# Layer norm statistics with five small VectorE operations to a pair of batches, and the second bias by TensorE in 3 of 16 batches

## The chip, the core and the metric

The kernel runs on one core of a Trainium2 chip. The metric is the device time of one execution in microseconds. A core has TensorE (PE, with its weight loads listed as PEld), VectorE (DVE), ScalarE (ACT), GpSimd (POOL) and SyncE (SP, which issues nearly all of the DMAs here). They run at the same time, each through its own list of instructions in order, and wait for each other through semaphores.

## What is computed

There are 128 batches of 128 rows with 512 columns, float32. Each batch has a language id 0 to 8, which picks its weights and its bias rows:

```
h = relu(x @ W1[id] + b1[id])          # 512 -> 128
y = x + h @ W2[id] + b2[id]            # 128 -> 512
n = (y - mean(y)) * rsqrt(var(y) + 1e-5)
out = x + n * gamma[id] + beta[id]
```

## The kernel before

At the start all weights are loaded into SBUF, and the rows of beta, gamma and b2 are spread over the 128 partitions: the rows lie as bfloat16 parts in `parts`, a column of the 0/1 tile `pick` selects one, a matmul copies it to all partitions (`spread`), and VectorE or ScalarE copies the result into `beta_b`, `gamma_b` and `b2_b`.

Then one iteration `i` of the main loop works on several batches at once, each in another stage. The order of each engine's instructions is the order of the calls (`keep` forbids a change).

- TensorE: `transpose_x(i)` (4 instructions, L191), `down(i-1)` (8, L214), `up(i-2)` (2, L231). Where `b2_by_matmul` holds, `up` has one more bfloat16 matmul ahead (L230) that puts the b2 row into the same accumulation.
- ScalarE: copies the transposed x out of PSUM (`copy_xT`, L195), copies the batch's W1 to a fixed place (`stage_w1`, L186), `relu` (L222), the sum of squares (`square`, L249), and once in two batches the square root (`deviation`, L255).
- GpSimd: `add_b2(b+2)` makes r = x + b2 (L201) where TensorE doesn't add b2, and `add_beta(b)` makes o = x + beta (L208). Here b = i - 3. GpSimd reads and writes SBUF in both.
- VectorE, three long instructions to a batch: `residual` adds x or r to the result in PSUM and gives the row sum (L237), `scale` computes (y - mean) * gamma in place (L281), `finish` computes o + y * rstd (L290).

VectorE has small instructions between them. Batches are handled in pairs `g` (even batch, odd batch), and the statistics of a pair have two columns. To a pair there are two times `negative_mean` (L242, one column each), and five instructions for 1/sqrt (L260, L264, L267, L270, L275): the reciprocal of ScalarE's square root and one Newton step. Intermediate results of these lie in PSUM (`stat`), others in SBUF.

Buffers tie the engines together. `p_y` has five PSUM tiles: `up(n)` waits until `finish(n-5)` has read its tile. `rp` has four tiles for r: `add_b2` waits for the `residual` that frees one. `op` has five pairs of o, freed by the stores. `xp` has four groups of four batches of x.

The last batches, from b = 124, are written out by hand in `tail`: statistics by single batch (`rstd_of`, `deviation_of`), part of the last step on ScalarE and GpSimd (`by_pool`, with `shift`, L334, a VectorE product of two SBUF columns), and stores of single batches.

Of the kernel before, what the change touches and what calls it, by code (L numbers as in the profile page):

```python
# [8 lines left out]
FP = mybir.dt.float32  # L9
# [14 lines left out]
def cond_resid_kernel(ctx: ExitStack, tc: tile.TileContext, x, itok, W1, b1, W2, b2, gamma, beta, out):  # L24
# [97 lines left out]
    nc.vector.tensor_scalar(lang, lang, 0, L - 1, ALU.max, ALU.min)  # L122


    R = 3 * L
    parts = const.tile([P, H], BF, name="parts")
    nc.vector.memset(parts.bitcast(mybir.dt.uint32), 0)
# [1 line left out]
    both = st.tile([P, R], FP, tag="both", name="both", bufs=1)[:96, :]  # L129
    nc.vector.tensor_tensor(both, ident[:96, 0:R], ident[:96, 32 : 32 + R], ALU.add)  # L130
    nc.vector.tensor_tensor(pick, both, ident[:96, 64 : 64 + R], ALU.add)
    left = rp.tile([P, H], FP, tag="r", name="left")
    nc.vector.tensor_copy(parts[0:R, :], rows[0:R, :])
    nc.vector.tensor_tensor(left[32 : 32 + R, :], rows[0:R, :], parts[0:R, :], ALU.subtract)
# [43 lines left out]
        return lids[g, engine][b % G]  # L178

    def b2_by_matmul(b):  # L180
        return b < 4 or b % 4 == 1

    def stage_w1(b):
        w1s[b] = wp.tile([P, KC, A], FP, tag="w1s", name=f"w1s_{b}")
# [12 lines left out]
    def add_b2(b):  # L197
        if not b2_by_matmul(b):
            rs[b] = rp.tile([P, H], FP, tag="r", name=f"r_{b}")
            v = lid(b, ET.Pool)  # L200
            keep(nc.gpsimd.tensor_tensor(rs[b], xb(b), b2_b[:, bass.ds(v * H, H)], ALU.add))  # L201

    def add_beta(b):
        g, j = divmod(b, 2)
        if j == 0:
            os[g] = op.tile([P, 2, H], FP, tag="o", name=f"o_{g}")
        v = lid(b, ET.Pool)
        keep(nc.gpsimd.tensor_tensor(os[g][:, j, :], xb(b), beta_b[:, bass.ds(v * H, H)], ALU.add))  # L208
# [15 lines left out]
    def up(b):  # L224
# [6 lines left out]
        keep(nc.tensor.matmul(ys[b], lhsT=hT[b], rhs=w2[:, bass.ds(v * H, H)], start=not m, stop=True))  # L231
        del hT[b]

    def residual(b):
        r = xb(b) if b2_by_matmul(b) else rs.pop(b)
        s = st.tile([P, 1], FP, tag="sum", name=f"sum_{b}")
        keep(nc.vector.scalar_tensor_tensor(ys[b], ys[b], 1.0, r, ALU.mult, ALU.add, accum_out=s))  # L237
        sums[b] = s

    def negative_mean(b):  # L240
        nmeans[b] = st.tile([P, 1], FP, tag="nmean", name=f"nmean_{b}")
        keep(nc.vector.tensor_scalar(nmeans[b], sums.pop(b), -1.0 / H, None, ALU.mult))  # L242

    def square(b):
        g, j = divmod(b, 2)
        if j == 0:
            ssqs[g] = st.tile([P, 2], FP, tag="ssq", name=f"ssq_{g}")
        sq = tp.tile([P, H], FP, tag="sq", name=f"sq_{b}")
        keep(nc.scalar.activation(sq, ys[b], AF.Square, bias=nmeans[b], accum_out=ssqs[g][:, j : j + 1]))  # L249

    sds, y0s, stats = {}, {}, {}

    def deviation(g):
        sds[g] = st.tile([P, 2], FP, tag="sd", name=f"sd_{g}")
        keep(nc.scalar.activation(sds[g], ssqs[g], AF.Sqrt, bias=eps, scale=1.0 / H))  # L255


    def rstd_1(g):
        stats[g] = p_s.tile([P, 6], FP, tag="s", name=f"stat_{g}")
        keep(nc.vector.tensor_scalar(stats[g][:, 0:2], ssqs.pop(g), -0.5 / H, -0.5 * EPS, ALU.mult, ALU.add))  # L260

    def rstd_2(g):
        y0s[g] = st.tile([P, 2], FP, tag="y0", name=f"y0_{g}")
        keep(nc.vector.reciprocal(y0s[g], sds.pop(g)))  # L264

    def rstd_3(g):
        keep(nc.vector.tensor_tensor(stats[g][:, 2:4], stats[g][:, 0:2], y0s[g], ALU.mult))  # L267

    def rstd_4(g):
        keep(nc.vector.tensor_tensor(stats[g][:, 4:6], stats[g][:, 2:4], y0s[g], ALU.mult))  # L270

    def rstd_5(g):
        rstds[g] = st.tile([P, 2], FP, tag="rstd", name=f"rstd_{g}")
        keep(
            nc.vector.scalar_tensor_tensor(rstds[g], stats.pop(g)[:, 4:6], 1.5, y0s.pop(g), ALU.add, ALU.mult)  # L275
        )

    def scale(b):
        v = lid(b, ET.DVE)
        keep(  # L280
            nc.vector.scalar_tensor_tensor(  # L281
                ys[b], ys[b], nmeans.pop(b), gamma_b[:, bass.ds(v * H, H)], ALU.add, ALU.mult
            )
        )

# [11 lines left out]
    def on(b):  # L297
        return 0 <= b < B
# [6 lines left out]
    def rstd_of(b, n):  # L305

        if not ends:
            ends["t"] = p_s.tile([P, 32], FP, tag="s", name="stat_ends")
        t = ends["t"][:, 8 * (b % 4) : 8 * (b % 4) + 3]
        if n == 1:  # L310
            keep(nc.vector.tensor_scalar(t[:, 0:1], ssqs.pop(b), -0.5 / H, -0.5 * EPS, ALU.mult, ALU.add))  # L311
        elif n == 2:
            y0s[b] = st.tile([P, 1], FP, tag="y0", name=f"y0_{b}")
            keep(nc.vector.reciprocal(y0s[b], sds.pop(b)))  # L314
        elif n < 5:
            keep(nc.vector.tensor_tensor(t[:, n - 2 : n - 1], t[:, n - 3 : n - 2], y0s[b], ALU.mult))  # L316
        else:
            rstds[b] = st.tile([P, 1], FP, tag="rstd", name=f"rstd_{b}")
            keep(nc.vector.scalar_tensor_tensor(rstds[b], t[:, 2:3], 1.5, y0s.pop(b), ALU.add, ALU.mult))  # L319

    def deviation_of(b):
        ssq = st.tile([P, 1], FP, tag="ssq", name=f"ssq_{b}")
        sq = tp.tile([P, H], FP, tag="sq", name=f"sq_{b}")
        keep(nc.scalar.activation(sq, ys[b], AF.Square, bias=nmeans[b], accum_out=ssq))
        sds[b] = st.tile([P, 1], FP, tag="sd", name=f"sd_{b}")
        keep(nc.scalar.activation(sds[b], ssq, AF.Sqrt, bias=eps, scale=1.0 / H))
        ssqs[b] = ssq

    def rstd_col(b):
        return rstds[b] if b > E else rstds[b // 2][:, b % 2 : b % 2 + 1]  # L330

    def shift(b):
        ends[b] = st.tile([P, 1], FP, tag="shift", name=f"shift_{b}")
        keep(nc.vector.tensor_tensor(ends[b], nmeans.pop(b), rstd_col(b), ALU.mult))  # L334

    def by_pool(b, scaled):

# [16 lines left out]
    def tail(b):  # L354
        p = E // 2
        if b == E + 3:
            rstd_of(b - 2, 4)
        residual(b)
        if b == E + 1:
            rstd_1(p)  # L360
            rstd_2(p)
            negative_mean(b)
            rstd_3(p)
            scale(E - 1)
            rstd_4(p)
            rstd_5(p)
            shift(E)
            finish(E - 2)
            store(p - 1)
            deviation_of(b)  # L370
            by_pool(E, False)
        elif b == E + 2:
            negative_mean(b)
            rstd_of(b - 1, 1)
            rstd_of(b - 1, 2)
            finish_last(E - 1)
            store_last(E)
            rstd_of(b - 1, 3)
            deviation_of(b)
        elif b == E + 3:  # L380
            rstd_of(b - 2, 5)
            negative_mean(b)
            shift(b - 2)
            residual(b + 1)
            negative_mean(b + 1)
            by_pool(b - 2, False)
            store_last(b - 2)
            rstd_of(b - 1, 1)
            rstd_of(b - 1, 2)
            rstd_of(b - 1, 3)  # L390
            scale(b - 1)
            deviation_of(b)
            rstd_of(b - 1, 4)
            rstd_of(b - 1, 5)
            scale(b)
            deviation_of(b + 1)
            by_pool(b - 1, True)
            store_last(b - 1)
            rstd_of(b, 1)
            rstd_of(b, 2)  # L400
            rstd_of(b + 1, 1)
            rstd_of(b + 1, 2)
            rstd_of(b, 3)
            rstd_of(b + 1, 3)
            scale(b + 1)
            rstd_of(b, 4)
            rstd_of(b + 1, 4)
            rstd_of(b, 5)
            rstd_of(b + 1, 5)
            finish_last(b)  # L410
            finish_last(b + 1)

# [38 lines left out]
    for i in range(3, B + U):  # L451
# [23 lines left out]
        p = g - 1  # L475
        mine, old = 0 <= p < B // 2, 0 <= p - 1 < B // 2
        if b == E:
            for n in range(b + 3, B):
                add_b2(n)
            for n in range(b + 1, B):  # L480
                add_beta(n)
        if b > E:
            tail(b)
        elif half == 0:
            if on(b):
                residual(b)
            if mine:
                scale(2 * p)
            if on(b):
                negative_mean(b)  # L490
            if mine:
                rstd_1(p)
                rstd_2(p)
            if old:
                finish(2 * p - 1)
                store(p - 1)
            if mine:
                rstd_3(p)
        else:
            if on(b):  # L500
                residual(b)
            if mine:
                rstd_4(p)
                scale(2 * p + 1)
                rstd_5(p)
            if on(b):
                negative_mean(b)
            if mine:
                finish(2 * p)
        if 0 <= b <= E:  # L510
            square(b)
# [43 lines left out]
```

## Time and profile before

| | |
|---|---|
| median of 3 runs | 320.62 us (320.58 to 321.12) |
| profiled execution | 321.39 us, span 318.8 us, TensorE clock 0.987 |
| TensorE | busy 305.1 us, 96% of the span |
| VectorE | busy 300.7 us, 94% |
| ScalarE | busy 285.5 us, 90% |
| GpSimd | busy 280.6 us, 88% |
| DMA | 72.88 MB, 16 engines busy 66.4% by the main queue |

The span is the time from the first to the last instruction. The time of the execution is 2.6 us longer, since it takes in what lies around the span. The profiled execution was 0.77 us slower than the median.

A busy share counts the records' durations, and those of instructions that follow each other overlap: the next one starts before the last one's record ends. What an instruction costs its engine in a full queue is the distance from its start to the start of the next, which is shorter than its duration.

### The profile page before, as it was taken

The numbers are of one execution on the slowest core, as the hardware profiler recorded it, in microseconds if no ns is written. First come the engines' busy times: TensorE is split into PE (matmuls) and PEld (weight loads), VectorE is DVE, ScalarE is ACT, GpSimd is POOL, SyncE is SP. The second block draws the span as 40 slices with busy tenths as digits, with TensorE's granted clock in tenths as the row PEclk, the third lists the DMA queues.
The fourth block names the chain that finished last, engine by engine and source line by source line (L and its number), as shares of the span: only waits on it lengthen the run. The fifth ranks groups of instructions, "written<-read, shape, count | busy, mean of one in ns | idle before, by whom it ended". The sixth has DMA issues, their size and how long they took to land. (4 is left out here: it accounts for less than half of the span.)

```text
span 318.8 us, 7184 instructions
## 1 busy us (share of the span) xinstructions
PE 305.1 (96%) x1889; PEld 226.0 (71%) x1889; DVE 300.7 (94%) x1000; ACT 285.5 (90%) x721; POOL 280.6 (88%) x234
## 2 busy tenths in 40 slices
PE   8998999999999999999999999999999999999960
PEld 3475777777777777777777777777777777777730
DVE  5946999999999999999999999999999999999995
ACT  2686989999999999999999999999999999999972
POOL 1306999999999999999999999999999999999873
PEclk9999999999999999999999999999999999999995
DMA  7997577577766666678666676678766666633324
GB/s 204 317 386 288 198 262 254 214 264 263 221 231 212 223 246 232 228 264 263 247 215 213 217 244 231 223 265 264 245 210 215 224 241 228 226 135 133 129 112 156
DMA packets 40986, 72.88 MB, mean 229 GB/s; under 512 B 1737, under 2 KB 6868, under 8 KB 40946
## 3 DMA queue, kind: packets, MB, share of 16 engines
q1 hardware_dynamic: 40886, 72.38, 66.4%
q8 instruction: 15, 0.25, 0.3%
q14 instruction: 25, 0.20, 0.2%
q10 hardware_dynamic: 60, 0.05, 0.1%
HBM read 38.86 MB, written 33.55 MB: 227 GB/s over the span
## 5 line engine op out<-in xcount | busy, mean ns | idle before, releaser
L208 POOL TENSOR_TENSOR o<-x,beta_b 128x512 f32<-128x512 f32 x128 | 162.0, 1278 | 10.6 <-DVE beta_b L160 10.6
L201 POOL TENSOR_TENSOR r<-x,b_b 128x512 f32<-128x512 f32 x93 | 118.8, 1277 | 20.0 <-DMA x<-in_x_dram 12.1
L214 PE MATMUL ph<-xT,w1s 128*128 128x128 f32 x1024 | 135.7, 275 | 0.3 <-ACT w1s L186 0.2
L231 PE MATMUL py<-w,hT 128*128 x256 | 130.9, 593 | 0.2 <-DVE o L290 0.2
L214 PEld LDWEIGHTS ph<-xT,w1s 128*128 128x128 f32 x1024 | 124.6, 192 | 2.6 <-ACT hT L222 1.3
L191 PEld LDWEIGHTS pxT<-ident,x 128*128 128x128 f32 x512 | 63.9, 141 | 67.1 <-issue 43.4
L281 DVE SCALAR_TENSOR_TENSOR py<-py,nmean,gamma_b 128x512 f32<-128x512 f32 x126 | 94.7, 752 | 0.3 <-issue 0.3
L290 DVE SCALAR_TENSOR_TENSOR o<-py,rstd,o 128x512 f32<-128x512 f32 x122 | 90.4, 741 | 1.4 <-DVE nmean L242 0.5
L249 ACT ACTIVATE sq<-py,nmean 128x512 f32<-128x512 f32 x124 | 85.3, 688 | 4.5 <-DVE nmean L242 2.9
L195 ACT COPY xT<-pxT 128x512 f32<-128x512 f32 x128 | 73.8, 577 | 12.1 <-PE pxT L191 10.1
L186 ACT COPY w1s<-w 128x512 f32 x128 | 79.5, 622 | 0.2 <-DVE gamma_b L160 0.2
L191 PE MATMUL pxT<-ident,x 128*128 128x128 f32 x512 | 77.0, 273 | 0.9 <-ACT xT L195 0.7
L237 DVE SCALAR_TENSOR_TENSOR py<-py,r 128x512 f32<-128x512 f32 x93 | 64.7, 695 | 2.5 <-POOL r L201 0.6
L222 ACT ACTIVATE hT<-ph,b1T 128x128 f32<-128x128 f32 x128 | 47.6, 372 | 1.1 <-PE ph L214 1.0
L231 PEld LDWEIGHTS py<-w,hT 128*128 128x128 f32 x256 | 41.6, 192 | 2.9 <-issue 0.9
L237 DVE SCALAR_TENSOR_TENSOR py<-py,x 128x512 f32<-128x512 f32 x35 | 24.2, 692 | 3.7 <-PE py L231 3.7
L249 ACT ACTIVATION_READ_ACCUMULATOR sq<-py,nmean 128x1 f32 x124 | 25.2, 203 | 0.0
L255 ACT ACTIVATE sd<-ssq,eps 128x2 f32<-128x2 f32 x62 | 18.3, 296 | 2.1
L242 DVE TENSOR_SCALAR nmean<-sum 128x1 f32<-128x1 f32 x128 | 18.7, 146 | 0.2
L230 PE MATMUL py<-parts,pick 96*128 96x512 bf16 x35 | 13.3, 381 | 0.0
L237 DVE DVE_READ_ACCUMULATOR py<-py,r 128x1 f32 x93 | 13.1, 141 | 0.0
L270 DVE TENSOR_TENSOR stat<-stat,y 128x2 f32<-128x2 f32 x62 | 12.8, 206 | 0.0
(54 smaller groups left out, 117.7 us busy)
## 6 DMA issues: line engine op xcount, KB each, us to landing
x<-in_x_dram SPq DMA_DIRECT2D x31, 1024.0 KB, 6.1
out_dram<-o SPq DMA_DIRECT2D x61, 512.0 KB, 3.5
w<-in_L_cond_W_dram SPq DMA_DIRECT2D x4, 640.0 KB, 6.6
w<-in_L_cond_W_dram SPq DMA_DIRECT2D x2, 1280.0 KB, 11.5
out_dram<-o SPq DMA_DIRECT2D x6, 256.0 KB, 2.2
x<-in_x_dram SPq DMA_DIRECT2D x2, 512.0 KB, 3.9
rows<-in_L_cond_beta_dram ACTq DMA_DIRECT2D x1, 20.0 KB
rows<-in_L_cond_gamma_dram SPq DMA_DIRECT2D x1, 20.0 KB
```

What stands on the lines that cost most here:

```text
L186: keep(nc.scalar.copy(w1s[b].rearrange("p k a -> p (k a)"), src))
L191: keep(nc.tensor.transpose(pxs[b][:, k, :], xb(b)[:, k * P : (k + 1) * P], ident))
L195: keep(nc.scalar.copy(xT[b], pxs.pop(b)))
L201: keep(nc.gpsimd.tensor_tensor(rs[b], xb(b), b2_b[:, bass.ds(v * H, H)], ALU.add))
L208: keep(nc.gpsimd.tensor_tensor(os[g][:, j, :], xb(b), beta_b[:, bass.ds(v * H, H)], ALU.add))
L214: nc.tensor.matmul(phs[b], lhsT=w1s[b][:, k, :], rhs=xT[b][:, k, :], start=(k == 0), stop=(k == KC - 1))
L222: keep(nc.scalar.activation(hT[b], phs.pop(b), AF.Relu, bias=b1T[:, bass.ds(lid(b, ET.Activation), 1)]))
L231: keep(nc.tensor.matmul(ys[b], lhsT=hT[b], rhs=w2[:, bass.ds(v * H, H)], start=not m, stop=True))
L237: keep(nc.vector.scalar_tensor_tensor(ys[b], ys[b], 1.0, r, ALU.mult, ALU.add, accum_out=s))
L249: keep(nc.scalar.activation(sq, ys[b], AF.Square, bias=nmeans[b], accum_out=ssqs[g][:, j : j + 1]))
L281: nc.vector.scalar_tensor_tensor(ys[b], ys[b], nmeans.pop(b), gamma_b[:, bass.ds(v * H, H)], ALU.add, ALU.mult)
L290: nc.vector.scalar_tensor_tensor(o, ys.pop(b), rstds[g][:, j : j + 1], o, ALU.mult, ALU.add)
```

## The change

Mean, sum of squares and 1/sqrt are computed in another form.

- The sum of a pair goes to two columns of one tile, and `negative_means` makes both means in one instruction, a `tensor_scalar` on 128x2 from SBUF to SBUF, instead of two on 128x1.
- `square` takes the sum itself: it computes (sum - 512 y)^2, 512 squared times too large, so that the scale factors change and ScalarE's square no longer reads the mean.
- 1/sqrt takes one step of Heron: with s the square root from ScalarE and v the variance, 1 / (s + v / s), in four instructions (reciprocal, two `scalar_tensor_tensor`, reciprocal). The factor 2 that this lacks is put into gamma: its columns of `pick` are doubled by one more VectorE instruction at the start. The intermediate columns lie in PSUM, the result in SBUF.
- The order in `tail` is written anew for this.
- `b2_by_matmul` holds for b < 4 and for b % 16 in (1, 6, 11), instead of for b < 4 and b % 4 == 1. That is 27 of the 128 batches, before 35. GpSimd gets the other 101, before 93. One of the last r is made after the last o.

```diff
+    nc.vector.tensor_scalar(pick[:, L : 2 * L], pick[:, L : 2 * L], 2.0, None, ALU.mult)
...
     def b2_by_matmul(b):
-        return b < 4 or b % 4 == 1
+        return b < 4 or b % 16 in (1, 6, 11)
...
+    def col(tiles, b):
+        return tiles[b // 2][:, b % 2 : b % 2 + 1]
...
-    def negative_mean(b):
-        nmeans[b] = st.tile([P, 1], FP, tag="nmean", name=f"nmean_{b}")
-        keep(nc.vector.tensor_scalar(nmeans[b], sums.pop(b), -1.0 / H, None, ALU.mult))
+    def negative_means(g):
+        nmeans[g] = st.tile([P, 2], FP, tag="nmean", name=f"nmean_{g}")
+        keep(nc.vector.tensor_scalar(nmeans[g], sums[g], -1.0 / H, None, ALU.mult))
...
-        keep(nc.scalar.activation(sq, ys[b], AF.Square, bias=nmeans[b], accum_out=ssqs[g][:, j : j + 1]))
+                sq, ys[b], AF.Square, bias=col(sums, b), scale=-float(H), accum_out=col(ssqs, b)
...
     def rstd_1(g):
+        y0s[g] = p_s.tile([P, 6], FP, tag="s", name=f"stat_{g}")
+        keep(nc.vector.reciprocal(y0s[g][:, 0:2], sds[g]))
     def rstd_2(g):
+        keep(nc.vector.scalar_tensor_tensor(t[:, 2:4], ssqs.pop(g), EPS * H3, t[:, 0:2], ALU.add, ALU.mult))
     def rstd_3(g):
+        keep(nc.vector.scalar_tensor_tensor(t[:, 4:6], t[:, 2:4], 1.0 / H3, sds.pop(g), ALU.mult, ALU.add))
     def rstd_4(g):
+        rstds[g] = st.tile([P, 2], FP, tag="rstd", name=f"rstd_{g}")
+        keep(nc.vector.reciprocal(rstds[g], y0s.pop(g)[:, 4:6]))
-    def rstd_5(g):
...
```

The order on VectorE, before and after, each letter group one instruction (e: even batch of the pair, o: odd batch, "-" the pair before, "--" the one before that):

```
before, even: residual(e), scale(e-), nmean(e), rstd_1, rstd_2, finish(o--), rstd_3
before, odd:  residual(o), rstd_4, scale(o-), rstd_5, nmean(o), finish(e-)
after,  even: residual(e), scale(e-), rstd_1, rstd_2, finish(o--), rstd_3
after,  odd:  residual(o), rstd_4, nmeans(e and o), scale(o-), finish(e-)
```

More of the change, by code (lines that the diff above doesn't have):

```diff
@@ L232, in up @@
         del hT[b]
+    def col(tiles, b):
+        return tiles[b // 2][:, b % 2 : b % 2 + 1]
     def residual(b):
         r = xb(b) if b2_by_matmul(b) else rs.pop(b)
-        s = st.tile([P, 1], FP, tag="sum", name=f"sum_{b}")
-        keep(nc.vector.scalar_tensor_tensor(ys[b], ys[b], 1.0, r, ALU.mult, ALU.add, accum_out=s))
-        sums[b] = s
-    def negative_mean(b):
-        nmeans[b] = st.tile([P, 1], FP, tag="nmean", name=f"nmean_{b}")
-        keep(nc.vector.tensor_scalar(nmeans[b], sums.pop(b), -1.0 / H, None, ALU.mult))
+        if b % 2 == 0:
+            sums[b // 2] = st.tile([P, 2], FP, tag="sum", name=f"sum_{b // 2}")
+        keep(
+            nc.vector.scalar_tensor_tensor(ys[b], ys[b], 1.0, r, ALU.mult, ALU.add, accum_out=col(sums, b))
+        )
+    def negative_means(g):
+        nmeans[g] = st.tile([P, 2], FP, tag="nmean", name=f"nmean_{g}")
+        keep(nc.vector.tensor_scalar(nmeans[g], sums[g], -1.0 / H, None, ALU.mult))
     def square(b):
@@ L248, in square @@
         sq = tp.tile([P, H], FP, tag="sq", name=f"sq_{b}")
-        keep(nc.scalar.activation(sq, ys[b], AF.Square, bias=nmeans[b], accum_out=ssqs[g][:, j : j + 1]))
+        keep(
+            nc.scalar.activation(
+                sq, ys[b], AF.Square, bias=col(sums, b), scale=-float(H), accum_out=col(ssqs, b)
+            )
+        )
     sds, y0s, stats = {}, {}, {}
+    H3 = float(H) ** 3
     def deviation(g):
         sds[g] = st.tile([P, 2], FP, tag="sd", name=f"sd_{g}")
-        keep(nc.scalar.activation(sds[g], ssqs[g], AF.Sqrt, bias=eps, scale=1.0 / H))
+        keep(nc.scalar.activation(sds[g], ssqs[g], AF.Sqrt, bias=eps, scale=1.0 / H3))
     def rstd_1(g):
-        stats[g] = p_s.tile([P, 6], FP, tag="s", name=f"stat_{g}")
-        keep(nc.vector.tensor_scalar(stats[g][:, 0:2], ssqs.pop(g), -0.5 / H, -0.5 * EPS, ALU.mult, ALU.add))
+        y0s[g] = p_s.tile([P, 6], FP, tag="s", name=f"stat_{g}")
+        keep(nc.vector.reciprocal(y0s[g][:, 0:2], sds[g]))
     def rstd_2(g):
-        y0s[g] = st.tile([P, 2], FP, tag="y0", name=f"y0_{g}")
-        keep(nc.vector.reciprocal(y0s[g], sds.pop(g)))
+        t = y0s[g]
+        keep(nc.vector.scalar_tensor_tensor(t[:, 2:4], ssqs.pop(g), EPS * H3, t[:, 0:2], ALU.add, ALU.mult))
     def rstd_3(g):
-        keep(nc.vector.tensor_tensor(stats[g][:, 2:4], stats[g][:, 0:2], y0s[g], ALU.mult))
+        t = y0s[g]
+        keep(nc.vector.scalar_tensor_tensor(t[:, 4:6], t[:, 2:4], 1.0 / H3, sds.pop(g), ALU.mult, ALU.add))
     def rstd_4(g):
-        keep(nc.vector.tensor_tensor(stats[g][:, 4:6], stats[g][:, 2:4], y0s[g], ALU.mult))
-    def rstd_5(g):
         rstds[g] = st.tile([P, 2], FP, tag="rstd", name=f"rstd_{g}")
-        keep(
-            nc.vector.scalar_tensor_tensor(rstds[g], stats.pop(g)[:, 4:6], 1.5, y0s.pop(g), ALU.add, ALU.mult)
-        )
+        keep(nc.vector.reciprocal(rstds[g], y0s.pop(g)[:, 4:6]))
     def scale(b):
@@ L281, in scale @@
             nc.vector.scalar_tensor_tensor(
-                ys[b], ys[b], nmeans.pop(b), gamma_b[:, bass.ds(v * H, H)], ALU.add, ALU.mult
+                ys[b], ys[b], col(nmeans, b), gamma_b[:, bass.ds(v * H, H)], ALU.add, ALU.mult
             )
@@ L310, in rstd_of @@
         if n == 1:
-            keep(nc.vector.tensor_scalar(t[:, 0:1], ssqs.pop(b), -0.5 / H, -0.5 * EPS, ALU.mult, ALU.add))
+            keep(nc.vector.reciprocal(t[:, 0:1], sds[b]))
         elif n == 2:
[L313 to L316, printed above, removed]
+            keep(
+                nc.vector.scalar_tensor_tensor(t[:, 1:2], ssqs.pop(b), EPS * H3, t[:, 0:1], ALU.add, ALU.mult)
+            )
+        elif n == 3:
+            keep(nc.vector.scalar_tensor_tensor(t[:, 2:3], t[:, 1:2], 1.0 / H3, sds.pop(b), ALU.mult, ALU.add))
         else:
             rstds[b] = st.tile([P, 1], FP, tag="rstd", name=f"rstd_{b}")
-            keep(nc.vector.scalar_tensor_tensor(rstds[b], t[:, 2:3], 1.5, y0s.pop(b), ALU.add, ALU.mult))
+            keep(nc.vector.reciprocal(rstds[b], t[:, 2:3]))
     def deviation_of(b):
@@ L323, in deviation_of @@
         sq = tp.tile([P, H], FP, tag="sq", name=f"sq_{b}")
-        keep(nc.scalar.activation(sq, ys[b], AF.Square, bias=nmeans[b], accum_out=ssq))
+        keep(nc.scalar.activation(sq, ys[b], AF.Square, bias=col(sums, b), scale=-float(H), accum_out=ssq))
         sds[b] = st.tile([P, 1], FP, tag="sd", name=f"sd_{b}")
-        keep(nc.scalar.activation(sds[b], ssq, AF.Sqrt, bias=eps, scale=1.0 / H))
+        keep(nc.scalar.activation(sds[b], ssq, AF.Sqrt, bias=eps, scale=1.0 / H3))
         ssqs[b] = ssq
@@ L333, in shift @@
         ends[b] = st.tile([P, 1], FP, tag="shift", name=f"shift_{b}")
-        keep(nc.vector.tensor_tensor(ends[b], nmeans.pop(b), rstd_col(b), ALU.mult))
+        keep(nc.vector.tensor_tensor(ends[b], col(nmeans, b), rstd_col(b), ALU.mult))
     def by_pool(b, scaled):
@@ L356, in tail @@
         if b == E + 3:
-            rstd_of(b - 2, 4)
+            rstd_of(b - 2, 3)
         residual(b)
@@ L361, in tail @@
             rstd_2(p)
-            negative_mean(b)
+            scale(E - 1)
             rstd_3(p)
-            scale(E - 1)
             rstd_4(p)
-            rstd_5(p)
             shift(E)
@@ L372, in tail @@
         elif b == E + 2:
-            negative_mean(b)
+            negative_means(b // 2)
             rstd_of(b - 1, 1)
@@ L377, in tail @@
             store_last(E)
-            rstd_of(b - 1, 3)
             deviation_of(b)
         elif b == E + 3:
-            rstd_of(b - 2, 5)
-            negative_mean(b)
+            rstd_of(b - 2, 4)
             shift(b - 2)
             residual(b + 1)
-            negative_mean(b + 1)
             by_pool(b - 2, False)
@@ L389, in tail @@
             rstd_of(b - 1, 2)
-            rstd_of(b - 1, 3)
+            negative_means(b // 2)
             scale(b - 1)
             deviation_of(b)
+            rstd_of(b - 1, 3)
             rstd_of(b - 1, 4)
-            rstd_of(b - 1, 5)
             scale(b)
@@ L401, in tail @@
             rstd_of(b + 1, 1)
+            rstd_of(b, 3)
             rstd_of(b + 1, 2)
-            rstd_of(b, 3)
-            rstd_of(b + 1, 3)
             scale(b + 1)
             rstd_of(b, 4)
+            rstd_of(b + 1, 3)
             rstd_of(b + 1, 4)
-            rstd_of(b, 5)
-            rstd_of(b + 1, 5)
             finish_last(b)
@@ L477, in cond_resid_kernel @@
         if b == E:
-            for n in range(b + 3, B):
-                add_b2(n)
+            add_b2(b + 3)
             for n in range(b + 1, B):
                 add_beta(n)
+            add_b2(b + 4)
         if b > E:
@@ L488, in cond_resid_kernel @@
                 scale(2 * p)
-            if on(b):
-                negative_mean(b)
-            if mine:
                 rstd_1(p)
@@ L503, in cond_resid_kernel @@
                 rstd_4(p)
+            if on(b):
+                negative_means(g)
+            if mine:
                 scale(2 * p + 1)
[L505 to L508, printed above, removed]
                 finish(2 * p)
```

## Prediction

> **What bounds the kernel now.** I read the table by stages first, since shares of the whole span mix head, loop and tail. Its columns are the stretch, then each engine's busy time in it.
>
> ```profile
> core 0: us, PE busy (x) PEld busy (x) DVE busy (x) ACT busy (x) POOL busy (x), PEclk, DMA share, GB/s
> 60.00:80.00 20.00, 19.98 (x128) 15.18 (x127) 19.31 (x64) 18.77 (x49) 20.00 (x17) 1.00 0.74 255
> 160.00:180.00 20.00, 20.00 (x128) 15.13 (x127) 19.85 (x69) 18.87 (x50) 19.46 (x17) 1.00 0.62 213
> 300.00:319.00 19.00, 8.02 (x43) 5.18 (x41) 14.95 (x57) 10.47 (x28) 11.78 (x10) 0.77 0.36 139
> ```
>
> All engines look full, so I need distances from start to start. The timeline gives them (start, duration, engine, line).
>
> ```profile
> 182.77 1.02 PE L231 MATMUL py<-w,hT 128*128 x2
> ...
> 183.78 1.29 POOL L208 TENSOR_TENSOR o<-x,beta_b 128x512 f32<-128x512 f32 x1
> ...
> 184.96 1.02 PE L231 MATMUL py<-w,hT 128*128 x2
> 185.01 1.29 POOL L201 TENSOR_TENSOR r<-x,b_b 128x512 f32<-128x512 f32 x1
> ...
> 187.15 0.38 PE L230 MATMUL py<-parts,pick 96*128 96x512 bf16 x1
> ...
> 187.37 1.02 PE L231 MATMUL py<-w,hT 128*128 x2
> ```
>
> A batch takes TensorE 2.19 us, and 0.22 more with the b2 matmul (187.37 - 187.15). Four batches, one with it, take 8.98 us (`up` of batch 77 to that of 105: 62.87 us for seven fours). **TensorE sets the pace**, without a gap. GpSimd is close: an instruction each 1.232 us (mean distance of those that follow without a wait; here 1.23). To 16 batches it has 28, 34.5 us against TensorE's 35.9; the rest is waiting for free r tiles, from 100 us on:
>
> ```profile
> POOL r L201 <- DVE py L237: 7.9, 23, 1.6
> ```
>
> VectorE, by distances in the loop: residual 0.616, scale 0.662, finish 0.65 us, small ones 0.06 to 0.07, or about 0.19 where one needs the result of the instruction just ahead (the tail's reciprocal at 309.93 and product at 310.12). A pair now needs about 4.38 us of the 4.49 that TensorE gives. After 302 us VectorE's chain alone sets the end.
>
> **What decides the forecast** is a thing that the loop doesn't show and the tail does: `shift` (L334), a VectorE product of two SBUF columns of 128x1, beside GpSimd.
>
> ```profile
> 300.54 4.96 POOL L208 TENSOR_TENSOR o<-x,beta_b 128x512 f32<-128x512 f32 x4
> ...
> 305.09 0.42 DVE L334 TENSOR_TENSOR shift<-nmean,rstd 128x1 f32<-128x1 f32 x1
> 305.44 0.74 DVE L290 SCALAR_TENSOR_TENSOR o<-py,rstd,o 128x512 f32<-128x512 f32 x1
> ...
> 307.82 1.26 POOL L344 TENSOR_TENSOR o<-n,o 128x512 f32<-128x512 f32 x1
> ...
> 308.86 0.23 DVE L334 TENSOR_TENSOR shift<-nmean,rstd 128x1 f32<-128x1 f32 x1
> ```
>
> GpSimd ends at 305.50 and 309.08; the shifts end at 305.51 and 309.09, both of them, after 0.42 and 0.23 us instead of some 0.15. They waited for GpSimd to finish.
>
> [...] L242 today has one column[...] and its 128 records take 0.131 to 0.157 us, with GpSimd nearly always busy: it never waits. The new `negative_means` has **two columns, SBUF to SBUF**[...].
>
> ```profile
> L242 DVE TENSOR_SCALAR nmean<-sum 128x1 f32<-128x1 f32 x128 | 18.7, 146 | 0.2
> ```
>
> **The change part by part.**
>
> *b2 by TensorE, 35 to 27 batches.* Up to batch 123, 34 become 27: 7 x 0.22 = 1.54 us less before the tail. TensorE then needs 16 x 2.19 + 3 x 0.22 = 35.71 us to 16 batches (4.464 to a pair).
>
> *The eight r on GpSimd.* 29 instructions, 29 x 1.232 = 35.73 us, level with TensorE; 0.02 x 7.5 blocks is 0.15 us. Its lead hides that: r is ready 5.4 to 6.3 us before its residual for batches 4 to 8, where today's queue then gains up to 9. The last r (batch 127) is GpSimd's 227th instruction after 26.61 us, so it ends near 306.2, just before its residual (309.0 now, some 2 earlier). Cost taken: 0; with the lead gone, every late GpSimd instruction would delay a residual. x groups are freed later where a matmul batch is the last of its group; SP's stores queue behind that load up to two batches (4.4 us), and o tiles have 10 batches. Taken: 0.
>
> *VectorE[...].* Two instructions go to a pair, and a nmean's successor no longer holds finish back; the second of the new four must await the first (0.19 for 0.07). Sum of a pair: 2 x (0.616 + 0.662 + 0.65) + 0.19 + 4 x 0.068 = 4.32 us. In the loop TensorE covers all of it: gain 0, margin 0.14. In the tail there is no cover: rstd ahead of batch 123's shift about 0.17 less, two means (0.14) and three Newton instructions of single batches (0.07 to 0.19 each) less; I take 0.6, between 0.2 and 1.0.
>
> *Square from the sum.* ScalarE's instruction keeps its shape (0.688 us) and is released earlier; ScalarE waits for TensorE's transposes (10.1 us in total), so 0. The odd residual writes the other column of the sum's tile; if that were made to wait for the even square, ScalarE ends it at 184.19 where the residual starts at 183.91, 0.3 us, of which the five PSUM tiles (finish to `up` 0.8 to 1.2 us spare) take all.
>
> *Doubling gamma.* One instruction, 0.19 us as L131 beside it, done at 6.45; the first spread matmul starts at 7.14. Cost 0, at most 0.2.
>
> Sum so far: 321.39 - 1.54 - 0.6 = 319.25 us, and 318.5 on the scale of the median, which is 0.77 lower.
>
> [...] `negative_means` [...] waits for the end of its instruction. Bounds for a wait: 0 and 1.23 us. Once it has started on such a boundary, the next one asks 4.32 us later, that is 4.32 / 1.232 = 3.5 GpSimd instructions[...]: a pair then takes 4 x 1.232 = 4.93 us. The margin of 0.14 can't hide a wait of 0.61; behind it stand scale, finish and the next residual, and after two or three pairs the five PSUM tiles are used up and `up` waits. 4.93 - 4.464 = 0.464 us, over the 60 pairs up to 123: **27.9 us**. Where GpSimd idles (it needs 3.625 instructions a pair, and would get 4) the phase starts anew, shorter if an even residual releases it, longer after an odd one. [...]
>
> 318.5 + 27.9 = **346.4 us**, from 326 to 362.
>
> **Rivals.** *No wait: faster.* [...] 318.5 (317 to 319.6). For it: no one-source instruction meets a busy GpSimd in this trace. Against it: [...] the two shifts. It decides at a mean wait of 0.14 us, VectorE's margin; above 0.18 us the gain of 2.1 us is lost ((0.18 - 0.14) x 60).
> *The queue starves the mean.* [...] the mean waits until GpSimd stands for an r tile: four instructions from the even residual's end, then scale, finish and residual, 6.9 us a pair, 5.7 where TensorE adds b2; mean 6.5, 318.5 + 2.0 x 60 = 439 us. The shifts met no such queue behind them.
> *GpSimd alone becomes the bound*, some per cent slower than 1.232 us with its lead gone: up to 322 to 325 us. Its steady distances (1.229 to 1.237) speak against it.
> *The gain is eaten* by late r and the head: within 0.2%.
>
> **Chances.** [...] starving 0.05, GpSimd alone 0.02: slower 0.67. No wait 0.29: faster. Eaten 0.04. 0.2%, 0.64 us, is about what a measurement here can tell from no change. The likeliest case's own range is 326 to 362; to leave out no more than two in ten it must reach the faster case: 317.6 to 362.
>
> **Signs.** Right: the row of `negative_means` (128x2, x64) has a mean near 0.75 us instead of 0.15, its ends coincide with ends of GpSimd's instructions; TensorE is busy 18 of 20 us in a stretch, its `up` waits for finish, GpSimd idles before r. The b2 row falls to x27, r rises to x101, the square waits less. Wrong: that row at 0.15 us, TensorE at 20.00 with a period of 2.19 and 2.41 us, and an end 2 us earlier.

## The result, and the profile after

The kernel after takes **364.48 us** in the median (362.12 to 367.86, 6 runs), the kernel before 320.71 us beside it (320.33 to 321.12, 6 runs). The ratio is 1.1335, with a 95% interval of 1.1300 to 1.1370: slower by 43.8 us, where 25.7 was forecast. The profiled execution took 364.79 us, its span is 363.0 us.

The table by stages (busy time of each engine in the stretch) shows where it went:

```profile
core 0: us, PE busy (x) PEld busy (x) DVE busy (x) ACT busy (x) POOL busy (x), PEclk, DMA share, GB/s
60.00:80.00 20.00, 19.40 (x122) 14.48 (x121) 19.82 (x55) 18.40 (x47) 18.49 (x16) 1.00 0.65 216
160.00:180.00 20.00, 16.75 (x99) 12.03 (x98) 19.83 (x48) 15.34 (x39) 17.92 (x16) 0.98 0.52 193
300.00:320.00 20.00, 19.31 (x122) 14.24 (x121) 19.82 (x53) 18.10 (x47) 16.46 (x14) 1.00 0.68 223
```

VectorE is "busy" all the time but finishes fewer instructions: 48 in the middle stretch where it had finished 69. GpSimd has lost busy time too. The groups of instructions say on what VectorE is busy (busy us, mean ns, idle before):

```profile
L203 POOL TENSOR_TENSOR r<-x,b_b 128x512 f32<-128x512 f32 x101 | 129.0, 1278 | 44.3 <-DVE py L245 32.0
...
L250 DVE TENSOR_SCALAR nmean<-sum 128x2 f32<-128x2 f32 x64 | 56.5, 883 | 0.7
```

The two-column mean takes 0.883 us in place of some 0.15. The wait lies inside the record, not in the idle column, which shows 0.7 us. The waits of the others follow from it (us in total, times, longest):

```profile
POOL r L203 <- DVE py L245: 32.0, 15, 2.9
ACT sq L259 <- DVE py L245: 30.6, 35, 4.5
...
PEld py L233 <- DVE o L302: 18.3, 31, 2.9
...
PE py L232 <- DVE o L302: 16.3, 9, 4.4
PE py L233 <- DVE o L302: 12.1, 24, 2.7
```

TensorE's `up` waits for `finish` (L302), and GpSimd for an r tile that a residual (L245) must free. The timeline shows two means, a usual one and a long one (start, duration, engine, line):

```profile
166.59 2.50 POOL L210 TENSOR_TENSOR o<-x,beta_b 128x512 f32<-128x512 f32 x2
...
168.47 0.65 DVE L250 TENSOR_SCALAR nmean<-sum 128x2 f32<-128x2 f32 x1
169.05 1.27 POOL L203 TENSOR_TENSOR r<-x,b_b 128x512 f32<-128x512 f32 x1
...
172.75 1.26 POOL L210 TENSOR_TENSOR o<-x,beta_b 128x512 f32<-128x512 f32 x1
...
173.39 3.09 DVE L250 TENSOR_SCALAR nmean<-sum 128x2 f32<-128x2 f32 x1
173.98 1.26 POOL L203 TENSOR_TENSOR r<-x,b_b 128x512 f32<-128x512 f32 x1
175.21 1.25 POOL L210 TENSOR_TENSOR o<-x,beta_b 128x512 f32<-128x512 f32 x1
...
178.54 1.27 POOL L203 TENSOR_TENSOR r<-x,b_b 128x512 f32<-128x512 f32 x1 [2.08 <-DVE py L245]
```

The first mean starts at 168.47 and ends at 169.12, where GpSimd's instruction ends (166.59 + 2.50 = 169.09). That is the forecast wait, and the distance to the next mean is 4.92 us, four GpSimd instructions. The second starts at 173.39, 0.62 us before a boundary (the end of a GpSimd instruction), as the first did. It doesn't end at the boundary of 174.01, nor at that of 175.24, but at 176.48, behind that of 176.46, where GpSimd has nothing ready: its next r stands for the residual at 177.72, which itself is behind the mean. From this mean to the next it is 7.37 us. A VectorE instruction whose record stays open over further GpSimd instructions in this way is called starved below, and the instructions that GpSimd can do one after the other without a pause are its list.

Seven of the 64 means are like that: one of 5.54 us and six of 3.09 to 3.10. All others are below 1.0 us. Against an ordinary wait of 0.65 us the seven cost 5.54 + 6 x 3.09 - 7 x 0.65 = **19.5 us**. Without them the kernel would stand at 364.48 - 19.5 = 345.0 us, if they cost what they last.

### The profile page after: what moved, and what is told of

Read it like the earlier page. It is cut to its first block, busy times and chain, and to the rows that moved or that the text cites. A ratio compares the mean times of both kernels' runs of the same rounds, so it can differ in the third digit from the quotient of the medians.

```text
span 363.0 us, 7096 instructions
## 1 busy us (share of the span) xinstructions
PE 320.3 (88%) x1880; PEld 230.8 (64%) x1881; DVE 344.1 (95%) x871; ACT 291.3 (80%) x721; POOL 289.9 (80%) x242
## 4 chain that ended last, share of the span: by engine, by line
POOL 46%; issue 28%; PE 12%; DVE 9%; POOLq 3%; ACT 1%; DVEq 1%; ACTq 0%
POOL o L210 29%; POOL r L203 16%; PE py L233 3%; PE ph L216 3%; DVE py L245 3%; DVE py L293 2%; POOLq L170 2%; PE row L157 2%; PE idle L424 2%; PE pxT L193 2%; DVE o L302 1%; POOLq L203 1%; DVE stat L280 0%; DVE stat L284 0%; POOLq L210 0%
## 5 line engine op out<-in xcount | busy, mean ns | idle before, releaser
L210 POOL TENSOR_TENSOR o<-x,beta_b 128x512 f32<-128x512 f32 x128 | 162.3, 1277 | 20.2 <-DMA out_dram<-o 10.4
L203 POOL TENSOR_TENSOR r<-x,b_b 128x512 f32<-128x512 f32 x101 | 129.0, 1278 | 44.3 <-DVE py L245 32.0
L233 PE MATMUL py<-w,hT 128*128 x256 | 137.5, 620 | 12.4 <-DVE o L302 12.1
L216 PEld LDWEIGHTS ph<-xT,w1s 128*128 128x128 f32 x1024 | 127.7, 196 | 2.0 <-ACT hT L224 0.8
L259 ACT ACTIVATE sq<-py,sum 128x512 f32<-128x512 f32 x124 | 85.2, 687 | 31.1 <-DVE py L245 30.6
L197 ACT COPY xT<-pxT 128x512 f32<-128x512 f32 x128 | 74.0, 578 | 21.2 <-PE pxT L193 19.6
L302 DVE SCALAR_TENSOR_TENSOR o<-py,rstd,o 128x512 f32<-128x512 f32 x122 | 90.2, 739 | 0.0
L245 DVE SCALAR_TENSOR_TENSOR py<-py,r 128x512 f32<-128x512 f32 x101 | 69.3, 686 | 2.6 <-PE py L233 2.6
L250 DVE TENSOR_SCALAR nmean<-sum 128x2 f32<-128x2 f32 x64 | 56.5, 883 | 0.7
L232 PE MATMUL py<-parts,pick 96*128 96x512 bf16 x27 | 10.3, 383 | 16.3 <-DVE o L302 16.3
L259 ACT ACTIVATION_READ_ACCUMULATOR sq<-py,sum 128x1 f32 x124 | 24.6, 198 | 0.0
L245 DVE SCALAR_TENSOR_TENSOR py<-py,x 128x512 f32<-128x512 f32 x27 | 18.6, 689 | 3.6 <-PE py L233 3.5
L245 DVE DVE_READ_ACCUMULATOR py<-py,r 128x1 f32 x101 | 13.9, 137 | 0.0
L280 DVE SCALAR_TENSOR_TENSOR stat<-ssq,stat 128x2 f32<-128x2 f32 x62 | 10.3, 166 | 2.1
```

Of the source, the lines that this page charges most:

```text
L197: keep(nc.scalar.copy(xT[b], pxs.pop(b)))
L216: nc.tensor.matmul(phs[b], lhsT=w1s[b][:, k, :], rhs=xT[b][:, k, :], start=(k == 0), stop=(k == KC - 1))
L250: keep(nc.vector.tensor_scalar(nmeans[g], sums[g], -1.0 / H, None, ALU.mult))
L259: nc.scalar.activation(sq, ys[b], AF.Square, bias=col(sums, b), scale=-float(H), accum_out=col(ssqs, b))
L302: nc.vector.scalar_tensor_tensor(o, ys.pop(b), rstds[g][:, j : j + 1], o, ALU.mult, ALU.add)
```

## The experiments

### The wait alone: one dead instruction to a pair

Into the kernel before, behind `rstd_4`, one instruction whose result nobody reads. It has two columns in the first kernel, one in the second.

```diff
                 rstd_4(p)
+                extra = st.tile([P, 2], FP, tag="extra", name=f"extra_{p}")
+                keep(nc.vector.tensor_scalar(extra, sds_kept[:, 0:2], -1.0 / H, None, ALU.mult))
                 scale(2 * p + 1)
```

> The kernel before with one more VectorE instruction to a pair, behind rstd_4: a tensor_scalar of a constant 128x2 from SBUF to SBUF, whose result nobody reads. [...] it waits like the pair's mean, a pair takes 4.93 us where GpSimd's list is full, with some waits of 3 us and more: 345 to 365 us. [...] it costs VectorE 0.07 us a pair, inside its margin of 0.1: 320 to 322 us.

> As e7_extra2 with one column instead of two[...]. [...] no wait, 320 to 322 us. If any tensor_scalar from SBUF to SBUF at this place waits for GpSimd: as e7_extra2.

Measured: two columns 346.99 us (ratio 1.0835 [1.0814, 1.0855]), one column 323.59 us (1.0107 [1.0089, 1.0126]). The rows, of the first and of the second kernel:

```profile
L507 DVE TENSOR_SCALAR extra<-sds_kept 128x2 f32<-128x2 f32 x61 | 37.1, 608 | 0.0
```

```profile
L507 DVE TENSOR_SCALAR extra<-sds_kept 128x1 f32<-128x1 f32 x61 | 11.9, 195 | 0.0
```

A second column of one float makes this instruction 0.41 us longer in the mean (608 ns for 195) and the kernel 23.4 us slower. Nothing else of the change is in it, so **the wait for GpSimd is shown**, with a price of 26.5 us against before (320.47 us beside it), 23.4 of it for the second column. All but one of the waits end at GpSimd's first boundary, 0.02 to 0.03 us after it; the one exception, 3.31 us, is near the start. TensorE's granted clock was 0.988 in this run and 0.987 before, so the clock is not the reason.

The one-column kernel shows something else: 0.06 us more to a pair already cost 3.1 us. VectorE's time alone doesn't explain that, since the kernel of the last experiment does pairs with seven small operations in 4.38 us (median). In the trace ScalarE's square waits for the mean, 15.6 us in 60 times, before 2.9 us in 7. That this wait is the cause was not tested.

### Two means of one column

The kernel after, with the mean as two instructions of one column.

```diff
-        keep(nc.vector.tensor_scalar(nmeans[g], sums[g], -1.0 / H, None, ALU.mult))
+        for j in (0, 1):
+            keep(nc.vector.tensor_scalar(nmeans[g][:, j : j + 1], sums[g][:, j : j + 1], -1.0 / H, None, ALU.mult))
```

> The changed kernel with one edit: the two means of a pair are made by two instructions of one column each, at the same place. [...] the row stays near 0.15 us, TensorE is full again with a period of 2.19 and 2.41 us, and the time is 318.5 us (317.5 to 319.6), faster than before. Rival (the rest of the change costs the time: 29 GpSimd instructions to 16 batches, or the dependent chain of the Heron step, and the mean's row only shows where VectorE stood): still above 340 us.

Measured: 334.47 us (1.0441 [1.0421, 1.0461]), between the theory and its rival. The means wait no more (0.144 us each), but the 318.5 us of the prediction's sum without a wait are missed by 16 us. So that sum lacked something that has nothing to do with the mean.

### The b2 rows alone

The kernel before with the new `b2_by_matmul` and nothing else.

```diff
-        return b < 4 or b % 4 == 1
+        return b < 4 or b % 16 in (1, 6, 11)
```

> The kernel before with one edit: b2 by TensorE for b < 4 and b % 16 in (1, 6, 11). TensorE's sum says 1.54 us less up to batch 123 and up to 0.2 in the tail: 319.1 us (318.7 to 319.6), GpSimd's lead of 5 us never used up. If GpSimd, level with TensorE, becomes the bound: 321 to 324 us, with residual waiting for r.

Measured: 335.08 us (1.0445 [1.0423, 1.0466]), as much as the one before. An edit that I had costed at nothing on GpSimd and on SP's queue loses 14.7 us (320.41 us beside it). The waits name two places (the last line is of SP's queue):

```profile
POOL o L208 <- DMA out_dram<-o: 14.0, 7, 3.3
...
PE py L231 <- DVE o L290: 12.6, 6, 8.4
...
ACT n L340 <- DVE shift L334: 9.5, 2, 8.1
DVE py L237 <- POOL r L201: 7.8, 6, 3.2
```

```profile
SPq L67 <- POOL o L208: 168.9, 27, 10.6
```

**The first place is SP's list.** A load of an x group (L67) waits in it until GpSimd's last o of the old group is made: 168.9 us in 27 times, up to 10.6, where the prediction had allowed 4.4. Before, this wait was 8.0 us in 6 times, up to 2.8. Now GpSimd has 29 instructions to a block of 16 batches and no lead, and the stores that stand behind the load are issued late and land late: 7.1 us from issue to landing in the median, before 3.5.

```profile
85.83 9.01 SPq L67 DMA_DIRECT2D x<-in_x_dram  x2
94.92 2.91 SPq L294 DMA_DIRECT2D out_dram<-o  x3
...
103.93 1.28 POOL L208 TENSOR_TENSOR o<-x,beta_b 128x512 f32<-128x512 f32 x1 [3.34 <-DMA out_dram<-o]
```

For 9 us SP's list issues two loads and nothing else, then three stores within 3 us. The first of them lands 8.9 us after its issue, and GpSimd, which has stood for that tile for 3.34 us, goes on. This comes once in a block, GpSimd has no spare time to make it up, and r comes late.

**The second place is the tail:**

```profile
310.43 1.29 POOL L201 TENSOR_TENSOR r<-x,b_b 128x512 f32<-128x512 f32 x1
311.65 1.29 POOL L208 TENSOR_TENSOR o<-x,beta_b 128x512 f32<-128x512 f32 x1
...
312.27 8.01 DVE L334 TENSOR_TENSOR shift<-nmean,rstd 128x1 f32<-128x1 f32 x1
312.87 2.51 POOL L201 TENSOR_TENSOR r<-x,b_b 128x512 f32<-128x512 f32 x2
315.31 4.95 POOL L208 TENSOR_TENSOR o<-x,beta_b 128x512 f32<-128x512 f32 x4
320.20 0.74 DVE L290 SCALAR_TENSOR_TENSOR o<-py,rstd,o 128x512 f32<-128x512 f32 x1
```

The shift, a product of two SBUF columns of one float, waits 8.0 us, past the boundary at 312.94 and through six further GpSimd instructions, until the list is empty at 320.26. In the kernel before the same shift had met the last instruction of that list and had taken 0.42 us.

### The two places mended

The kernel with two one-column means, with seven pairs of o tiles instead of five; then also with a shift that reads only one operand as a tensor.

```diff
-    op = ctx.enter_context(tc.tile_pool(name="op", bufs=5))
+    op = ctx.enter_context(tc.tile_pool(name="op", bufs=7))
...
-        keep(nc.vector.tensor_tensor(ends[b], col(nmeans, b), rstd_col(b), ALU.mult))
+        keep(nc.vector.tensor_scalar(ends[b], col(nmeans, b), rstd_col(b), None, ALU.mult))
```

> The kernel with two one-column means (e1_split) and seven pairs of o tiles instead of five. If its loop is slow because GpSimd waits for stores that stand behind a load of x in SP's list, the seven waits of o for a store (15.7 us) go, r comes in time, and the loop from up(4) to up(123) falls from 276.4 to 266.3 us. The shift of batch 123 still waits for GpSimd's list to run empty, some 3 to 8 us: 321 to 326 us. If GpSimd's 29 instructions to 16 batches are too many by themselves, the loop stays above 272 us with residual waiting for r.

> As e5_split_o7, and shift as a tensor_scalar of the mean's column with rstd as its per-partition scalar, so that it has one SBUF tensor input. If the shift's wait is that of a second SBUF input, it takes 0.16 us and the tail is 15.5 to 16.3 us: 317.5 to 319.5 us, faster than before by 0.3 to 0.9%. If a scalar column counts as an input as well, the shift still waits and the time is that of e5_split_o7.

Measured: 321.78 us (1.0045 [1.0029, 1.0060]) with the tiles, 320.86 us (1.0013 [1.0007, 1.0020]) with both. With the tiles the wait for o is gone, and 12.7 of the 13.6 us: GpSimd is ahead again, so that the shift too meets the last instruction of a list. These are the shift of the first kernel and that of the second, each started about 1.0 us before GpSimd's instruction ends:

```profile
305.93 1.01 DVE L348 TENSOR_TENSOR shift<-nmean,rstd 128x1 f32<-128x1 f32 x1
```

```profile
306.01 0.21 DVE L348 TENSOR_SCALAR shift<-nmean,rstd 128x1 f32<-128x1 f32 x1
```

As a `tensor_scalar` it takes 0.21 us where the product took 1.01: it doesn't wait. Both causes are shown, the lack of o tiles and the shift; that the tiles were lacking because of SP's order is read from the trace, and no run changed that order. What is left is that the 1.5 us which TensorE saves aren't had. By distances from start to start VectorE's pair is now 2 x (0.606 + 0.666 + 0.660) + 0.222 for the means + 0.198 + 0.074 + 0.067 + 0.081 = 4.506 us, more than TensorE's 4.464.

### The mean in PSUM

The kernel after with the two-column mean written to PSUM; all small columns then lie in one PSUM tile, `small`.

```diff
-        nmeans[g] = st.tile([P, 2], FP, tag="nmean", name=f"nmean_{g}")
+        nmeans[g] = small_psum(64 + 2 * (g % 4), 66 + 2 * (g % 4))
```

> The changed kernel with its two-column mean written to PSUM instead of SBUF (all small PSUM columns in one tile), still one instruction. [...] no wait, 318.5 us or slightly less than with two instructions (317.5 to 319.3). If what waits is the one SBUF read beside a busy GpSimd, whatever the output: above 340 us.

Measured: 339.90 us (1.0613 [1.0598, 1.0627]).

```profile
L257 DVE TENSOR_SCALAR small<-sum 128x2 f32<-128x2 f32 x64 | 10.5, 164 | 2.2
```

The same two columns no longer wait: 0.164 us in the mean with the result in PSUM, 0.883 with it in SBUF, and none above 0.165 us. The time is lost elsewhere:

```profile
202.10 0.76 DVE L300 SCALAR_TENSOR_TENSOR py<-py,small,gamma_b 128x512 f32<-128x512 f32 x1
202.97 0.17 DVE L283 RECIPROCAL small<-sd 128x2 f32<-128x2 f32 x1
...
204.98 0.77 DVE L300 SCALAR_TENSOR_TENSOR py<-py,small,gamma_b 128x512 f32<-128x512 f32 x1
205.65 0.74 DVE L309 SCALAR_TENSOR_TENSOR o<-py,rstd,o 128x512 f32<-128x512 f32 x1
```

Ahead of `finish` a scale costs 0.67 us, ahead of the reciprocal, which writes the tile that this scale reads, 0.87. `rstd_4` ahead of the mean and the mean ahead of the scale cost 0.20 each. The pair is 4.81 us on VectorE, 0.31 more than with two one-column means in SBUF, which is 18 us over 60 pairs. The place in which the mean doesn't wait made its neighbours dearer.

### The mean in another place

The kernel after with the mean behind the second scale of its pair instead of ahead of it.

```diff
-            if on(b):
-                negative_means(g)
             if mine:
                 scale(2 * p + 1)
+            if on(b):
+                negative_means(g)
+            if mine:
                 finish(2 * p)
```

> The changed kernel with the two-column mean moved behind scale(2p+1), so that the odd residual frees an r tile 0.7 us before the mean asks, not just before. If the seven waits of 3 us and more come from the r instruction which that residual releases at the same moment, they go, waits are 0 to 1.25 us, a pair takes 4.93 us or less and the time is 340 to 350 us. If they come from GpSimd's queue being full, whatever the moment, they stay: 358 to 368 us.

Measured: 356.96 us in the median, but the four times lie between 347.82 and 357.96, so it is no sharp number. The profiled execution (357.43) has two long waits, of 4.4 us, instead of seven, and longer ordinary ones (0.75 to 1.28 us). Inconclusive on the cause: in this one trace fewer means are starved, but the price hardly falls.

### The wait with the b2 rows of before

The kernel after with `b < 4 or b % 4 == 1` again.

> The kernel after with the b2 rows of the kernel before (35 batches by TensorE instead of 27; GpSimd's list has 7 instructions to two pairs again instead of 29 to eight). Everything else of the change stays: the two-column mean, the square from the sum, the one step of Heron. Theory: the change costs [...] (26.5 us, measured by one dead two-column instruction to a pair in the kernel before), and the rest of the 43.9 us comes from the long waits (3.1 to 5.5 us), which the thinner b2 set brings. Then 345 to 350 us, the means at 0.3 to 1.2 us, and at most two of 64 over 2 us. Rival: the long waits come from where the new order puts the mean, or from the small operations around it, whatever the b2 set: 358 to 368 us with five or more waits over 2 us.

Measured: 343.27 us (1.0703 [1.0661, 1.0745]), a little below the forecast 345 to 350.

```profile
L250 DVE TENSOR_SCALAR nmean<-sum 128x2 f32<-128x2 f32 x64 | 36.3, 567 | 0.7
```

The mean falls from 883 to 567 ns. One of the 64 is long (6.75 us, near the start); all others are at most 0.88 us, regularly 0.31 and 0.65 in turn. The b2 rows cost 14.7 us alone and 21.2 us on top of the wait, but not for the same reason: of the 21.2 us, 13.4 are what the long waits last beyond 0.65 us (19.5 us with the new rows, 6.1 with the old ones). The theory holds for the larger part, and the rest is not explained.

### Six r tiles

The kernel after with `rp` at six tiles instead of four, so that GpSimd has more work ready.

> The kernel after with six r tiles instead of four, so that GpSimd's b2 instruction seldom stands for an r tile that a residual must free. Theory: a mean waits through several GpSimd instructions when the odd residual ahead of it has just released a b2 instruction that stood for its r tile; with tiles to spare no release falls there, the seven waits over 2 us go, and the time is 347 to 354 us with waits of 0.3 to 1.3 us. Rival: a request that meets a list of GpSimd instructions that are all ready is starved until the list runs empty, as the shift in the tail was (8.0 us through six instructions); with more r tiles the list is longer, the long waits are as many or longer, and the time is 364 to 390 us.

Measured: between 362.03 and 392.25 us in four runs (median 377.12). The profiled one is the fastest, and its trace has four waits over 1.35 us, of 7.97, 4.32, 6.75 and 1.87 us. The longest:

```profile
55.44 7.97 DVE L250 TENSOR_SCALAR nmean<-sum 128x2 f32<-128x2 f32 x1
57.23 1.28 POOL L203 TENSOR_TENSOR r<-x,b_b 128x512 f32<-128x512 f32 x1
58.45 1.27 POOL L210 TENSOR_TENSOR o<-x,beta_b 128x512 f32<-128x512 f32 x1
59.67 1.28 POOL L203 TENSOR_TENSOR r<-x,b_b 128x512 f32<-128x512 f32 x1
60.89 1.27 POOL L210 TENSOR_TENSOR o<-x,beta_b 128x512 f32<-128x512 f32 x1
62.11 1.27 POOL L203 TENSOR_TENSOR r<-x,b_b 128x512 f32<-128x512 f32 x1
64.38 1.27 POOL L210 TENSOR_TENSOR o<-x,beta_b 128x512 f32<-128x512 f32 x1 [1.00 <-DMA out_dram<-o]
```

The mean ends at 63.41, where GpSimd's instruction of 62.11 ends (63.38) and the next one stands for an o tile. My theory, that the release of a b2 instruction brings the long wait, falls. The rival holds in its main point: the starved means ended where GpSimd's list did, and with more tiles the longest took 7.97 us, where it had taken 5.54. The long waits are fewer, though (four for seven).

### One mean that doesn't wait

The kernel after with both mends, and the mean of a pair as one product of the sums with two columns of -1/512 that stay in PSUM.

```diff
-        keep(nc.vector.tensor_scalar(nmeans[g], sums[g], -1.0 / H, None, ALU.mult))
+        keep(nc.vector.tensor_tensor(nmeans[g], sums[g], small_psum(64, 66), ALU.mult))
```

> The kernel after with the two means of a pair still in one instruction, but as a tensor_tensor of the sums in SBUF with two columns of -1/H kept in PSUM, written to SBUF; seven o tiles instead of five; the shift of the tail as a tensor_scalar with its factor from a column. [...] scale reads its mean from SBUF at its old 0.66 us. VectorE's pair is then 4.506 us (measured with two one-column means) less 0.22 for those and plus 0.11 to 0.17 for this one: 4.40 to 4.45 us, under TensorE's 4.464. Theory: TensorE sets the pace and the time is 318.3 to 319.5 us, faster than the kernel before by 0.3 to 0.7%. Rival: VectorE still sets the pace since the instruction costs more than 0.17 us start to start: 320.2 us or more. Rival: [...] 345 us or more.

Measured: 320.36 us, ratio 0.9993 [0.9977, 1.0008]: no difference from before. The mean doesn't wait (0.156 us each). But VectorE's pair is 4.505 us, as with two means:

```profile
202.37 0.17 DVE L296 RECIPROCAL rstd<-small 128x2 f32<-128x2 f32 x1
202.55 0.16 DVE L258 TENSOR_TENSOR nmean<-sum,small 128x2 f32<-128x2 f32 x1
202.68 0.76 DVE L301 SCALAR_TENSOR_TENSOR py<-py,nmean,gamma_b 128x512 f32<-128x512 f32 x1
```

`rstd_4` now costs 0.178 us start to start, for the mean behind it needs the sum that the residual just ahead has left. The mean costs 0.128, for the scale behind it needs the mean. The two one-column means and their `rstd_4` had cost 0.303, these two cost 0.306.

### The b2 rows with the mends, and nothing else

The kernel before with the new `b2_by_matmul`, seven pairs of o tiles and the shift as a `tensor_scalar`. The seven small operations stay.

> The kernel before with only the b2 rows of the change (3 of 16 batches by TensorE), plus the two repairs: seven o tiles instead of five, and the shift of the tail as a tensor_scalar with its factor from a column. Without the repairs this edit cost 14.3 us. Theory: all of that came from the stores behind loads on SP's queue, which took o tiles from GpSimd, and from the shift starved in the tail; with both gone the 1.54 us of TensorE's work come out: 318.9 to 319.6 us. Rival: VectorE's seven small operations to a pair have no room for a shorter TensorE pair (a dead instruction of 0.06 us to a pair cost 2.9 us), so that nothing is gained: 320.2 to 321.0 us. Rival: GpSimd's 29 instructions in 16 batches are the bound themselves: 322 us or more.

Measured: **318.83 us** (318.69 to 319.13), ratio 0.9936 [0.9913, 0.9960], the fastest of all these kernels.

```profile
160.00:180.00 20.00, 20.00 (x129) 15.17 (x128) 19.74 (x69) 19.17 (x49) 20.00 (x17) 1.00 0.65 221
```

TensorE and GpSimd are both busy for 20.00 of 20 us. The gain of 1.7 us is near the forecast 1.54 of TensorE's b2 matmuls; what part of it is the shift of the tail was not separated. VectorE's seven small operations fit, and by the distances in this trace they are the cheaper form: 0.20 us for two means (with what they wait) and 0.072 + 0.071 + 0.071 + 0.066 + 0.061 for the rest, 0.54 us to a pair. The five of the change cost 0.65.

## Why the prediction was right or wrong

**Right: the sign, and the wait of the mean.** The two-column `tensor_scalar` from SBUF to SBUF ended with the GpSimd instruction that it met in 55 of 64 cases, 0.02 to 0.03 us after it; two met none and took 0.16 and 0.17 us, seven are the long ones. That it would was the author's estimate, put at 0.60: the trace of before had shown such a wait for the two shifts, another kind of instruction (0.42 and 0.23 us). One column more in an instruction whose result nobody reads showed the price (23.4 us, against the 27.9 of the prediction's step). The regular pair is four GpSimd instructions, 4.92 to 4.93 us, as worked out. Most signs came: ends that coincide with GpSimd's, `up` behind `finish`, GpSimd idle ahead of r, x27 and x101. One did not: the square waits more, 31.1 us in place of 4.5, for it now stands for residuals that come late. The row's mean is 0.883 us where 0.75 was written; without what the long waits last beyond 0.65 us it would be 0.58.

**Wrong: 4.93 us, four GpSimd instructions, for every pair.** Seven means didn't end at the first boundary after their start but where GpSimd's list stood. They cost 19.5 us, and the forecast was short by 364.48 - 346.4 = 18.1. That the rest of its sum was nearly right is luck, two errors of opposite sign: without this wait and the others the kernel stands at 320.9 us (the two means split and the two places mended), not at 318.5, and the ordinary waits cost 345.0 - 320.9 = 24.1 us, not 27.9. The rival "the queue starves the mean" had such waits in it, and was put at 0.05 with 439 us, since it was taken for all pairs or none. A run mixes both. The trace of before could have warned: its two shifts met no queue behind them, as the prediction says itself, so they were no evidence on what happens with one. In the traces of five kernels (after, the dead two-column instruction, the late mean, the b2 rows of before, six r tiles) there are 15 such waits, and each of them ended where GpSimd's next instruction wasn't ready, none at a boundary within the list.

**A line of before that was overlooked.** For the faster rival the prediction says that no one-source instruction meets a busy GpSimd in the trace of before. The one-column L242 does, as it says itself elsewhere, and so does one with two columns:

```profile
L264 DVE RECIPROCAL y<-sd 128x2 f32<-128x2 f32 x62 | 9.6, 156 | 0.2 <-ACT sd L255 0.2
```

It has two columns, SBUF on both sides, 61 of its 62 records lie within one of GpSimd's, and none takes more than 0.20 us. So two columns and one source weren't enough for a wait: the runs show it for `tensor_scalar` (0.883 us) and show none for this reciprocal (0.156 us).

**Wrong: "Taken: 0" for SP's stores and the o tiles.** In the kernel before with the b2 rows alone it cost 14.7 us. Its profiled execution is 7.1 us longer in the loop, from `up(4)` to `up(123)`, and 8.4 behind it, where the late GpSimd list starved the shift. "Up to two batches (4.4 us)" was an estimate from today's order; with GpSimd level with TensorE the load waited 10.6. In the kernel after itself GpSimd waits for o tiles 10.4 us, and the mean's wait probably hides most of it, as VectorE is slower still. That is not shown, since no run had the two-column mean with seven pairs of o tiles.

**Wrong: the tail's gain of 0.6.** From `up(123)` to the last computation the kernel before takes 16.23 us and the kernel after 16.99, with one mean there waiting 0.88 us. With the means split and the shift mended it is 15.83, 0.4 us less. The kernel before with the same shift and the new b2 rows (last experiment) has 15.84, so that the shorter statistics show no gain there. The shift served the prediction as evidence, and its own wait was not priced for a fuller GpSimd list: with the b2 rows alone it cost 8.0 us.

**Wrong: VectorE's "margin 0.14".** The sum of 4.32 us took one dependent step of 0.19 and four of 0.068; the measured small operations of a pair cost 0.645 instead of 0.46, and the pair 4.505. Three of the five, not one, stand ahead of an instruction that needs what is just being made (0.199, 0.178, 0.128). So without the wait, and with the two places mended, the change gains nothing (320.86 us with two means, 320.36 with one), where 318.5 was forecast: the faster rival was wrong for a reason of its own.

**Not shown: a cost of each mean to GpSimd.** Both ends of the range, 326 and 362, counted one. In the trace of after GpSimd's distance from start to start is 1.231 us in the median for the 47 instructions that a mean preceded at the boundary, and 1.231 for those without one (its records last 1.277): a two-column mean costs GpSimd nothing that the trace shows. So the range ended at 362 for the wrong reason, and still fell 2.5 us short.

**Open:** what decides whether such an instruction ends at the next boundary. A starved one and one that wasn't can look alike: start 0.62 us ahead of the boundary, the same two instructions of GpSimd on either side. One thing sets the 15 apart in the traces of the five kernels: ahead of the GpSimd instruction that they met, at least nine others had followed each other without a pause (9 to 23). Of the 243 that met a busy GpSimd after fewer than nine, none was starved; of the 50 after nine or more, 15 were. So all 15 came after a long stretch without a pause, and 35 others that came after one ended at the next boundary. It fits that long waits are rare where GpSimd pauses often (one of 64 with the b2 rows of before, one of 61 with the dead instruction), but no run changed this alone.

## What to carry to other kernels

Before two small VectorE operations are merged into one wider one, measure whether the wider form waits for another engine (here 0.144 us with one column, 0.883 with two), and price the wait by that engine's whole ready list (up to 8.0 us here), not only by the rest of its instruction (0.65 us), above all where that engine seldom pauses. Count small operations by what stands behind them: here one that its successor needed cost 0.13 to 0.20 us, the others 0.06 to 0.08. And GpSimd, brought level with TensorE, lost its lead, which cost 14.7 us: everything that such a lead had kept early (stores, tiles, a last operation in the tail) has to be priced anew.

## What the runs showed of the hardware

- A two-column `tensor_scalar` from SBUF to SBUF usually ended with GpSimd's running instruction, 0.02 to 0.03 us after it (0.65 us for the mean of 168.47); in 15 cases it did not, and then it ended only where GpSimd had no instruction ready, 1.9 to 8.0 us after its start. In these the rest of GpSimd's list ran while it was open.
- The number of columns made the difference for this `tensor_scalar` of float32 from SBUF to SBUF: 128x1 took 0.131 to 0.157 us in the kernel before (128 records) and 0.144 in the mean in the changed one, 128x2 there 0.883; the dead instruction took 0.195 with one column and 0.608 with two. 128x2 with PSUM as destination (0.164 us), or as a `tensor_tensor` with its second source in PSUM (0.156 us), didn't wait, and neither did a reciprocal of 128x2 from SBUF to SBUF (0.156 us).
- A product of two SBUF columns of 128x1 was starved in the same way (8.0 us, behind a stretch of 16 GpSimd instructions without a pause), and the same product as a `tensor_scalar` with its factor from a column took 0.21 us where the product took 1.01, both started some 1.0 us ahead of the end of GpSimd's instruction.
